# Attention and group norm of an audio tower kept transposed, and its planner re-priced

## The chip, the cores and the metric

The kernel runs on one core of one Trainium2 chip. The metric is the device time of one execution in microseconds (us), the median of three executions. Engines are named as in the profile: PE (matrix multiply), PEld (its weight loads), DVE (vector), ACT (activation functions), POOL, and SP, which only issues DMAs.

## The reference

A batch of 32 signals of 160000 samples is cut into 313 frames of 512 (a DCT turns each frame into 512 features). Then one layer of retention-like attention with a residual, and one feed-forward part (FFN) that sums sines and cosines, with a residual.

```python
h = frames @ dct.T                                   # 32 x 313 x 512
X = layernorm(h)
Q, K, V = xpos(X @ W_Q), xpos(X @ W_K), X @ W_V      # 8 heads of 64
p = softmax(Q @ K.T) * Dmat                          # Dmat: decay gamma ** |n - m|
Y = p @ V
Yn = (Y - mean(Y)) * rsqrt(var(Y) + 1e-5)            # group norm: over the 64 of one head
h = h + (silu(X @ W_G) * (Yn * gn_weight + gn_bias)) @ W_O
x = layernorm(h)
theta = x[..., None, :] / (1 + abs(W)) + B_param     # 256 units x 512 features
sin, cos = 4096-entry tables at round(theta * 4096 / 2pi)
out = (cos * attn_cos).sum(-1) @ proj_cos.T + (sin * attn_sin).sum(-1) @ proj_sin.T
h = h + silu(out)
```

The FFN needs a sine and a cosine for each of 32 x 313 x 256 x 512 arguments. That is the bulk of the work, and ACT computes them all (L636).

## The kernel before, in words

**The FFN.** Two sequences form a pair, and 16 pairs pass through a ring. The 256 units are 8 blocks of 32, and a *round* (`ffn_round`, L574) takes one block for all pairs that are in the ring. Pair p enters at round `STARTS[p]` (L33) and stays for 8 rounds, so rounds hold one to four pairs, that is r = 2 to 8 sequences; 42 rounds are needed. I call a round's share of one pair a pair-round; there are 16 x 8 = 128. A round has 128 items (32 units x 4 chunks of 128 features), and `SLOT` = 24 sequences' worth of items make one *slot*: for r = 2, 4, 6, 8 a slot takes 12, 6, 4 or 3 items. In a slot DVE makes integer table indices, one instruction an item (L612), shifts them by a quarter turn (L621) and masks both sets (L628). ACT takes two sines of 7512 elements (L636, tile `trig`, two buffers). After each sine PE does 24 matmuls with a 32-column stationary matrix `hot` into four column groups of a PSUM bank (`pa`, L658), summing over features. At a round's end DVE copies the banks out (`part`, L675) and SP stores them. The index tile `ix` has five buffers. The normalized input of the FFN goes through DRAM (`xT_d`) and is loaded per chunk into `xT` (two buffers).

**Attention** (`attention`, L302) handles one sequence at a time in one set of buffers (`A`); the first two sequences run side by side ahead of the FFN, in `A` and `B`. Frames are three overlapping tiles of 105 (`NT` = 3, `ROW0`). Stages: DCT rows (`rows`, L275), layer norm with an inverse root by Newton steps on POOL (`rsqrt`, L221: seed on DVE, 12 operations on POOL), transposes, values V into `x.h`, and Q, K with rotation per pair of heads (`rotary`). Then scores per head: PE, maximum and subtraction on DVE (L382, L385). One exponential follows over all heads (L400), or, where the FFN is narrow, 24 small ones with sums on ACT (L404). Then each head's 9 transposes into PSUM (L428), the decay product by DVE (L440), and PV: 9 matmuls a head, the probabilities stationary, 64 columns of V moving (L446), so that Y lies with frames on the partitions; per two heads a copy to `x.h` (L460). The group norm squares Y (L481, or L478 on ACT), sums per head on DVE (L486), makes the variance (L488 to L491), takes the root on POOL, and multiplies it in on DVE (L498). Y is transposed by PE (L269) and gets weight and bias (L509), is multiplied with the gate (L514), and goes through W_O (`rows`, L515) to the residual (L517) and the second norm. `output` (L528) finishes a sequence after its 8 rounds: rows with the projections, silu (L547), residual (L550). In narrow phases ACT instead of DVE does the copies (`eng`).

**What sets the order.** Nothing is ordered by the source order itself. Every step is given to `Plan.add` (L56) with a key, an engine, a price in ns, and the buffers read and written. `emit` (L63) walks through the engines in the planner's own time: an operation is ready when its forerunners have ended by their prices (plus `WAIT` 300, and `LAND` 2500 after a DMA), and of the ready ones of an engine that with the lowest key is issued. The resulting queues are fixed, and each engine goes through its own in order. Keys count slots: an FFN slot's key is its number (`key_of`, L794), its table loads stand 4 to 10 earlier. A sequence's attention is spread over a stretch of keys `times[i]` to `times[i+1]` that ends 8 slots before its pair enters (L797 to L804); within it the function `step` places each stage by a share of the whole (L309). A wrong price therefore puts an instruction too early or too late in a queue.

Of the kernel before, what the change touches and what calls it, by code (L numbers as in the profile page):

```python
# [15 lines left out]
AF = mybir.ActivationFunctionType  # L16
ALU = mybir.AluOpType
# [4 lines left out]
P = 128  # L22
HOP = 512
# [4 lines left out]
EPS = 1e-5  # L28
RING = 8
# [3 lines left out]
STARTS = (0, 4, 8, 10, 12, 14, 16, 18, 20, 22, 24, 26, 28, 30, 32, 34)  # L33
# [93 lines left out]
def tile_audio_tower(ctx: ExitStack, tc: tile.TileContext, t: dict, out: bass.AP):  # L127
# [23 lines left out]
    class Buffers:  # L151


        def __init__(self, name, pool, psum):
# [16 lines left out]
            self.h = sb("h", NT, HOP)  # L171
            self.xnT = sb("xnT", NC4, S)
# [11 lines left out]
            self.sq = wide[:, : NT * HOP].rearrange("p (i d) -> p i d", d=HOP)  # L184
            self.hres = self.sq
            self.aff = wide[:, NT * HOP : NT * HOP + NC4 * S].rearrange("p (c s) -> p c s", s=S)
# [8 lines left out]

            self.y = self.W[:, 3, : NT * 2 * DH].rearrange("p (i d) -> p i d", d=2 * DH)
# [24 lines left out]
    def rsqrt(plan, key, val, r, u, kv, kr, ku):  # L221
# [17 lines left out]
        plan.add(key, "POOL", 6000, newton, (kv,), (kr, ku))  # L239
# [24 lines left out]
    def transposed(plan, key, x):  # L264

        for c in range(NC4):
            def go(c=c):
                for i in range(NT):
                    nc.tensor.transpose(  # L269
                        x.W[:, c, ROW0[i] : ROW0[i] + N], x.h[:N, i, c * P : (c + 1) * P],  # L270
                        ident[:N, :N],
                    )
            plan.add(key, "PE", 800, go, x.rows_of, x.banks(c))

    def rows(plan, key, x, lhsT, src, r, order=range(NT), src_r=()):  # L275

        for c in range(NC4):
            k = x.load(plan, key, src[c], src_r)
            for to, i in enumerate(order):
                plan.add(  # L280
                    key, "PE", 880,
# [7 lines left out]
    def columns(plan, key, x, bank, src):  # L289
# [4 lines left out]
        for c in range(NC4):  # L294
            plan.add(
                key, "PE", 550,
# [5 lines left out]
    def attention(plan, keys, sq, x, eng, swap_m=None):  # L302
# [6 lines left out]
        def step(n=1.0):  # L309
            done[0] += n  # L310
            return keys(done[0] / 135.0)
# [14 lines left out]
        plan.add(step(0), "SP", DMA_NS, lambda: nc.sync.dma_start(x.u, t["frames"][sq]), (), us)  # L326
        rows(plan, step(7), x, x.u, t["dct"], us)
        copy(plan, step(), eng, NT * HOP, x.h[:N], W3, x.banks(0, 1, 2), hs)
        residual(step(0), False)
        layernorm(plan, step(3), x)  # L330
        transposed(plan, step(3), x)
        copy(plan, step(), eng, NC4 * S, x.xnT, x.W[:, :, :S], x.banks(0, 1, 2, 3), (x.k("xnT"),))


        rows(plan, step(7), x, x.xnT, wv_d, (x.k("xnT"),), range(NT - 1, -1, -1),
             ("wv_d",))
        copy(plan, step(), eng, NT * HOP, x.h[:N], W3, x.banks(0, 1, 2), hs)
        plan.add(step(0), "POOL", 500, lambda: nc.gpsimd.memset(x.h[0:1, : NT - 1, :], 0.0), (), hs)

        plan.add(step(0), "SP", DMA_NS, lambda: nc.sync.dma_start(x.table, t["turn_qk"]),  # L340
                 (), probs[-4:-2])

        def rotary(g):
            key = step(4)
# [7 lines left out]
            else:  # L352
                copy(plan, key, eng, 2 * S, x.raw, x.W[:, 0:2, :S], x.banks(0, 1), probs[-1:])
                for i in range(2):
                    plan.add(key, "PE", 550,
# [11 lines left out]
        def scores(hd):  # L367
            key = step(2.5)
            r0 = (hd % 2) * DH
            qk, kq = x.qk[hd // 2 % 2], x.k("u", hd // 2 % 2)  # L370
            for i in range(NT):
                plan.add(
                    key, "PE", 660,
# [34 lines left out]
        plan.add(step(2), "ACT", 18200 if eng == "ACT" else 9500, exps,  # L408
                 (), [*probs, x.k("sm"), x.k("lu")])
        if eng == "DVE":  # L410
            for a in range(0, H, 2):
                plan.add(step(0), "DVE", 2080,
# [4 lines left out]
        for hd in range(H):  # L417
            key = step(5)
# [4 lines left out]
            for jj in range(NT):  # L423
# [8 lines left out]
                plan.add(key, "PE", 800, go, (probs[a],), x.banks(jj))  # L432
# [10 lines left out]
            for i in range(NT):  # L443
                def go(i=i, hd=hd, a=a):
                    for jj in range(NT):
                        nc.tensor.matmul(  # L446
                            x.y[:N, i, (hd % 2) * DH : (hd % 2 + 1) * DH],
                            x.prob[:N, a, jj, ROW0[i] : ROW0[i] + N],
                            x.h[:N, jj, hd * DH : (hd + 1) * DH],
                            start=(jj == 0), stop=(jj == NT - 1),  # L450
                        )
                plan.add(key, "PE", 1000, go, (probs[a], hs[hd // 2]), x.banks(3))
            if hd % 2 == 0:
# [3 lines left out]
            h0 = hd - 1  # L457
            plan.add(
                step(), "DVE", 560,
                lambda h0=h0: nc.vector.tensor_copy(  # L460
                    x.h[:N, :, h0 * DH : (h0 + 2) * DH], x.y[:N]),
                x.banks(3), (hs[h0 // 2],),
            )


        key = step(6)
        for g in range(NC4):
            columns(plan, key, x, g, t["wg"][g])
        plan.add(step(), "ACT", 1270,
# [4 lines left out]
        xh = x.h[:N].rearrange("p i (h e) -> p (i h) e", e=DH)  # L474
        key = step(5)
        if eng == "ACT":
            plan.add(key, "ACT", 1500,
                     lambda: nc.scalar.activation(x.sq[:N], x.h[:N], AF.Square), hs, room)  # L478
        else:
            plan.add(key, "DVE", 1760,  # L480
                     lambda: nc.vector.tensor_tensor(x.sq[:N], x.h[:N], x.h[:N], ALU.mult),  # L481
                     hs, room)

        def variance():
            f = lambda tl: tl[:N].rearrange("p i h -> p (i h)")
            nc.vector.tensor_reduce(  # L486
                f(x.gv), x.sq[:N].rearrange("p i (h e) -> p (i h) e", e=DH), AX.X, ALU.add)
            nc.vector.reciprocal(f(x.sm), f(x.sm))  # L488
            nc.vector.tensor_tensor(f(x.gv), f(x.gv), f(x.sm), ALU.mult)
            nc.vector.tensor_tensor(f(x.gv), f(x.gv), f(x.sm), ALU.mult)  # L490
            nc.vector.tensor_scalar(f(x.gv), f(x.gv), 1.0 / DH, EPS, ALU.mult, ALU.add)  # L491
        plan.add(key, "DVE", 2700, variance, room, [x.k("gv"), x.k("sm")])
        rsqrt(plan, key, x.gv[:N], x.gr[:N], x.gu[:N], x.k("gv"), x.k("gr"), x.k("gu"))
        plan.add(key, "POOL", 300,
                 lambda: nc.gpsimd.tensor_tensor(x.gr[:N], x.gr[:N], x.sm[:N], ALU.mult),
                 (x.k("sm"),), (x.k("gr"),))
        plan.add(key, "DVE", 1760,
                 lambda: nc.vector.tensor_tensor(  # L498
                     xh, xh, x.gr[:N].rearrange("p i h -> p (i h)").unsqueeze(2).to_broadcast(
                         (N, NT * H, DH)), ALU.mult),  # L500
                 (x.k("gr"),), hs)


        transposed(plan, step(4), x)
        residual(step(0), True)
        key = step(2)
        for c in range(NC4):
            plan.add(key, "DVE", 530,
                     lambda c=c: nc.vector.tensor_scalar(  # L509
                         x.aff[:, c, :], x.W[:, c, :S], gnw[:, c : c + 1], gnb[:, c : c + 1],  # L510
                         ALU.mult, ALU.add),
                     x.banks(c), room)
        plan.add(key, "DVE", 1460,
                 lambda: nc.vector.tensor_tensor(x.u, x.u, x.aff, ALU.mult), room, us)  # L514
        rows(plan, step(7), x, x.u, t["wo"], us)  # L515
        plan.add(step(2), "DVE", 1760,
                 lambda: nc.vector.tensor_tensor(x.h[:N], x.h[:N], W3, ALU.add),  # L517
                 x.banks(0, 1, 2), hs)
        residual(step(0), False)
        layernorm(plan, step(3), x)  # L520
        transposed(plan, step(3), x)
        key = step()
# [51 lines left out]
    def ffn_round(plan, k0, blk, ring):  # L574
# [10 lines left out]
        for parts in slots:  # L585
# [45 lines left out]
            for k in (1, 0):  # L631
# [34 lines left out]
                plan.add(key, "PE", 150 * len(parts) * r, go,  # L666
# [32 lines left out]
    gnw = load("gnw", NC4)  # L699
# [128 lines left out]
def _constants(S):  # L828
# [35 lines left out]
    c["decay"] = dec.astype(f)  # L864
    return c
# [20 lines left out]
def _layout(x, W_Q, W_K, W_V, W_G, W_O, gn_weight, gn_bias, W, B_param, attn_cos, attn_sin, pc, psn):  # L886
# [14 lines left out]
    a["gnw"] = np.ascontiguousarray(gn_weight.reshape(NC4, P).T)  # L901
# [38 lines left out]
```

## Time and profile before

| | |
|---|---|
| times of three executions | 18586.4, 18587.15, 18591.35 us (median 18587.15) |
| profiled execution, its own time | 18593.15 us |
| its span, first to last instruction | 18591.2 us |
| sines (L636) | 2760, ACT busy 17398.1 us with them |
| FFN matmul records (L658) | 131072, two to a matmul |
| index, shift and mask (L612, L621, L628) | DVE busy 6499.2 + 2905.2 + 5581.8 us |
| granted PE clock, mean | 0.918 |

The page gives for each engine its busy time and its share of the span, then the same in 40 slices of 465 us, a digit being tenths of the slice. Groups of instructions are named by line, engine, operation, and `out<-in` with their tiles; after a count comes busy time and the mean of one in ns. A view by stage cuts the span where one asks and gives each engine's busy time with the number of its instructions in brackets, then granted PE clock, DMA share and GB/s. A line of waits reads: engine, what it was about to do, what released it, then us in total, times, and the longest.

### The profile page before, as it was taken

To read this page: it belongs to the slowest core of one execution; us is meant where nothing else is said; L and a number is where in the kernel's file an instruction comes from. 1 tells how busy PE (TensorE), PEld (TensorE's weight loads), DVE (VectorE), ACT (ScalarE), POOL (GpSimd) and SP (SyncE) were. 2 spreads that over 40 slices of the span, in tenths; PEclk is the share of its full clock that TensorE was granted. 3 is DMA by queue.
4 is the path that set the end of the run, shared out by engine and by line. 5 is a ranking of instruction groups with operands and counts; after the bars stand their busy time and mean duration, and the time that the engine had idled before them with its cause. 6 is when DMAs were issued, how large, how long until landed. Compare 5 with 4: busy or idle time off the path is not lost. (4 is left out here: it accounts for less than half of the span.)

```text
span 18591.2 us, 325962 instructions
## 1 busy us (share of the span) xinstructions
PE 14520.5 (78%) x148768; PEld 6791.6 (37%) x148768; DVE 17165.7 (92%) x11210; ACT 17827.2 (96%) x3248; POOL 968.9 (5%) x1222
## 2 busy tenths in 40 slices
PE   8788888888777877778877787877788777666666
PEld 5443333334333333333333333333333333222222
DVE  6989999999999999999999999999999999888887
ACT  4899999999999999999999999999999999999998
POOL 0000000000000000000000000000000000000000
PEclk8899999999999999999999999999999999888888
DMA  3221121121111111111111111111111111001011
GB/s 94 71 66 56 60 67 58 54 61 58 45 38 47 57 50 52 45 45 57 48 58 47 43 53 48 58 48 55 39 50 57 48 56 42 29 21 33 20 40 53
DMA packets 598691, 942.55 MB, mean 51 GB/s; under 512 B 116768, under 2 KB 337952, under 8 KB 586048
## 3 DMA queue, kind: packets, MB, share of 16 engines
q1 hardware_dynamic: 597312, 921.70, 16.0%
q8 instruction: 1166, 19.10, 0.4%
q14 instruction: 213, 1.74, 0.0%
HBM read 816.78 MB, written 104.66 MB: 50 GB/s over the span
## 5 line engine op out<-in xcount | busy, mean ns | idle before, releaser
L636 ACT ACTIVATE trig<-ix 128x7512 f32<-128x7512 int16 (+1 forms) x2760 | 17398.1, 6386 | 456.8 <-PE pa L658 229.7
L658 PE MATMUL pa<-trig,hot 128*32 128x313 f32 x131072 | 10304.5, 468 | 3545.1 <-ACT trig L636 3530.3
L658 PEld LDWEIGHTS pa<-trig,hot 128*32 128x32 f32 x131072 | 4291.2, 118 | 9312.4 <-ACT trig L636 4578.4
L612 DVE TENSOR_SCALAR ix<-xT,f 128x2504 int16<-128x2504 f32 (+3 forms) x5376 | 6499.2, 1268 | 431.6 <-ACT trig L636 389.4
L628 DVE TENSOR_SCALAR ix<-ix 128x15024 int16<-128x15024 int16 (+4 forms) x1656 | 5581.8, 3385 | 41.1
L621 DVE TENSOR_SCALAR ix<-ix 128x7512 int16<-128x7512 int16 (+1 forms) x1380 | 2905.2, 2105 | 356.1 <-ACT trig L636 264.4
L297 PE MATMUL a_W<-a_xnT,a_ring 128*128 128x313 f32 x4896 | 1426.2, 437 | 40.9 <-DVE a_prob L385 15.4
L282 PE MATMUL a_W<-a_ring,a_u 128*105 128x512 f32 x2256 | 1087.5, 625 | 141.2 <-DMA a_u<-in_frames 52.9
L297 PEld LDWEIGHTS a_W<-a_xnT,a_ring 128*128 128x128 f32 x4896 | 891.8, 190 | 580.1 <-issue 212.5
L282 PEld LDWEIGHTS a_W<-a_ring,a_u 128*105 128x105 f32 x2256 | 374.7, 177 | 756.3 <-issue 615.0
L233 POOL TENSOR_TENSOR a_gu<-a_gr 105x24 f32<-105x24 f32 x93 | 104.5, 1124 | 9461.6 <-DVE a_gr L227 9456.7
L446 PE MATMUL a_W<-a_h,a_prob 105*105 105x64 f32 x4464 | 483.0, 264 | 77.6 <-DVE a_prob L440 77.4
L374 PE MATMUL a_W<-a_u 64*105 64x313 f32 x1488 | 477.7, 453 | 72.1 <-DVE a_prob L385 40.0
L446 PEld LDWEIGHTS a_W<-a_h,a_prob 105*105 105x105 f32 x4464 | 447.3, 177 | 212.1 <-issue 143.7
L282 PE MATMUL a_W<-a_ring,a_xnT 128*105 128x512 f32 x744 | 350.6, 611 | 22.3 <-DVE a_xnT L219 20.5
L233 POOL TENSOR_TENSOR a_lu<-a_lr 105x3 f32<-105x3 f32 x186 | 141.1, 759 | 4073.3 <-DVE a_lr L227 4063.6
L374 PEld LDWEIGHTS a_W<-a_u 64*105 64x105 f32 x1488 | 234.0, 171 | 310.8 <-DVE a_prob L385 79.2
L428 PE MATMUL a_W<-ident,a_prob 105*105 105x105 f32 x2232 | 284.9, 272 | 44.1 <-DVE a_h L460 26.1
L382 DVE TENSOR_REDUCE a_mx<-a_W 105x3 f32<-105x939 f32 x248 | 280.1, 1130 | 37.6 <-PE a_W L374 36.5
L428 PEld LDWEIGHTS a_W<-ident,a_prob 105*105 105x105 f32 x2232 | 237.9, 178 | 159.4 <-issue 92.5
L440 DVE TENSOR_TENSOR a_prob<-a_W,a_u 105x939 f32<-105x939 f32 x248 | 279.8, 1128 | 16.3 <-PE a_W L428 10.9
L385 DVE TENSOR_TENSOR a_prob<-a_W,a_mx 105x939 f32<-105x939 f32 x248 | 281.7, 1136 | 8.5
(134 smaller groups left out, 3386.8 us busy)
## 6 DMA issues: line engine op xcount, KB each, us to landing
hot<-in_hot SPq DMA_DIRECT2D x1344, 128.0 KB
xT<-xT_d SPq DMA_DIRECT2D x88, 1252.0 KB
a_u<-in_decay SPq DMA_DIRECT2D x248, 260.5 KB
a_ring<-in_proj SPq DMA_DIRECT2D x128, 256.0 KB
a_ring<-in_dct SPq DMA_DIRECT2D x124, 256.0 KB
a_ring<-wv_d SPq DMA_DIRECT2D x124, 256.0 KB
a_ring<-in_wq SPq DMA_DIRECT2D x124, 256.0 KB
a_ring<-in_wk SPq DMA_DIRECT2D x124, 256.0 KB
```

Of the source, the lines that this page charges most:

```text
L282: lambda c=c, i=i, k=k, to=to: nc.tensor.matmul(x.W[:N, to, :], lhsT[:, c, ROW0[i] : ROW0[i] + N], x.ring[k], start=(c == 0), stop=(c == N ...
L297: lambda c=c: nc.tensor.matmul(x.W[:, bank, :S], w[:, c, :], x.xnT[:, c, :], start=(c == 0), stop=(c == NC4 - 1)),
L374: lambda i=i: nc.tensor.matmul(x.W[:N, i, :S], qk[r0 : r0 + DH, 0, ROW0[i] : ROW0[i] + N], qk[r0 : r0 + DH, 1, :], start=True, stop=True,),
L382: lambda: nc.vector.tensor_reduce(m[:N], x.W[:N, :NT, :S], AX.X, ALU.max),
L385: lambda: nc.vector.tensor_tensor(x.prob[:N, hd], x.W[:N, :NT, :S], m[:N].unsqueeze(2).to_broadcast((N, NT, S)), ALU.subtract),
L428: nc.tensor.transpose(x.W[:N, jj, ROW0[i] : ROW0[i] + N], x.prob[:N, a, i, ROW0[j] : ROW0[j] + N], ident[:N, :N],)
L446: nc.tensor.matmul(x.y[:N, i, (hd % 2) * DH : (hd % 2 + 1) * DH], x.prob[:N, a, jj, ROW0[i] : ROW0[i] + N], x.h[:N, jj, hd * DH : (hd + 1) ...
L612: nc.vector.tensor_scalar(ix[:, x[0], pt * r * S : (pt + 1) * r * S], now["xT", y][:, : r * S], f[:, 0, n : n + 1], f[:, 1, n : n + 1], AL ...
L621: nc.vector.tensor_scalar(ix[:, x[1], :E], ix[:, x[0], :E], float(LUT // 4), None, ALU.add)
L628: nc.vector.tensor_scalar(ix[:, i, :E], ix[:, i, :E], LUT - 1, LUT // 2, ALU.bitwise_and, ALU.bitwise_xor)
L636: nc.scalar.activation(tl[:, :E], ix[:, x[1 - k], :E], AF.Sin, bias=-PI32, scale=ANG)
L658: nc.tensor.matmul(now["pa", p][g * 32 : g * 32 + 32, :S], now["hot", hot[n // 4 * 4, c]][:, n % 4, k, :], now["trig", w][:, s0 : s0 + S], ...
```

## The change

Three things change together.

**Attention keeps Y transposed.** V is stored by pairs of heads (`x.v`). After both heads of a pair have their decayed probabilities, 6 matmuls make their result: V (105 x 64) is stationary, the probabilities (313 frames wide) move, and the two heads go to columns 0 to 63 and 64 to 127 of one PSUM bank. The copy (`x.yT`, 128 x 313) thus has features on the partitions. The group norm's sums come from PE with a 0/1 table `of_head` (12 matmuls, 8 columns wide). Two DVE operations make the variance, the softmax sum folded into the epsilon term. The root is computed on POOL as before, then PE transposes it (3), DVE copies it (8 x 313), and PE spreads it over the features with `head_w`, which holds `gn_weight` (4 matmuls). DVE multiplies, and adds the bias and multiplies the gate in one operation for each of 4 chunks. One of the three rounds of 12 transposes goes, and `gnw` too; two small tables are loaded per sequence.

**The planner's numbers.** The steps' shares come from `SHARE` and `TIMES`; prices change: Newton 6000 to 7500, three transposes 800 to 400, row matmuls 880 to 970, column matmuls 550 to 600, scores 660 to 640, the memset 500 to 2000. The FFN's PE operations get a key lower by 1.

**`STARTS`** changes, so that 43 rounds are needed.

```diff
+SHARE = dict(rows=5.0, copy=2.5, norm=8.0, turn=0.7, rotary=4.2, scores=3.2, exps=2.0, head=3.5,
+             pair=0.8, gate=4.1, silu=1.5, group=7.0, affine=5.0)
+TIMES = dict(rows=3, copy=5, norm=2, turn=4, rotary=4, scores=8, exps=1, head=8, pair=4, gate=1,
+             silu=1, group=1, affine=1)
+WHOLE = sum(SHARE[k] * TIMES[k] for k in SHARE)
...
-STARTS = (0, 4, 8, 10, 12, 14, 16, 18, 20, 22, 24, 26, 28, 30, 32, 34)
+STARTS = (0, 4, 7, 9, 11, 13, 15, 17, 19, 21, 23, 25, 27, 29, 32, 35)
...
+            self.v = flat.rearrange("p (g j d) -> p j g d", g=NC4, j=NT)
+            self.yT = flat.rearrange("p (g s) -> p g s", g=NC4)[:, :, :S]
...
-        plan.add(key, "POOL", 6000, newton, (kv,), (kr, ku))
+        plan.add(key, "POOL", 7500, newton, (kv,), (kr, ku))
...
-            plan.add(key, "PE", 800, go, x.rows_of, x.banks(c))
+            plan.add(key, "PE", 400, go, x.rows_of, x.banks(c))
...
-        def step(n=1.0):
-            done[0] += n
-            return keys(done[0] / 135.0)
+        def step(stage=None):
+            if stage:
+                done[0] += SHARE[stage]
+            return keys(done[0] / WHOLE)
...
-                plan.add(key, "PE", 800, go, (probs[a],), x.banks(jj))
+                plan.add(key, "PE", 400, go, (probs[a],), x.banks(jj))
...
-            for i in range(NT):
-                def go(i=i, hd=hd, a=a):
-                    for jj in range(NT):
-                        nc.tensor.matmul(
-                            x.y[:N, i, (hd % 2) * DH : (hd % 2 + 1) * DH],
-                            x.prob[:N, a, jj, ROW0[i] : ROW0[i] + N],
-                            x.h[:N, jj, hd * DH : (hd + 1) * DH],
-                            start=(jj == 0), stop=(jj == NT - 1),
-                        )
-                plan.add(key, "PE", 1000, go, (probs[a], hs[hd // 2]), x.banks(3))
...
+            def go(g=hd // 2):
+                for jj in range(NT):
+                    for b in range(2):
+                        nc.tensor.matmul(
+                            x.W[b * DH : (b + 1) * DH, 3, :S],
+                            x.v[:N, jj, g, b * DH : (b + 1) * DH],
+                            x.prob[:N, 2 * g + b, jj, :], start=(jj == 0), stop=(jj == NT - 1))
+            plan.add(key, "PE", 1900, go, (*probs[hd - 1 : hd + 1], hs[hd // 2]), x.banks(3))
+            plan.add(step("pair"), "DVE", 550,
+                     lambda g=hd // 2: nc.vector.tensor_copy(x.yT[:, g, :], x.W[:, 3, :S]),
+                     x.banks(3), (hs[hd // 2],))
...
-                     lambda: nc.vector.tensor_tensor(x.sq[:N], x.h[:N], x.h[:N], ALU.mult),
+                     lambda: nc.vector.tensor_tensor(x.sqT, x.yT, x.yT, ALU.mult), hs, room[:2])
+        def sums():
+            for i in range(NT):
+                for c in range(NC4):
+                    nc.tensor.matmul(x.W[:N, 0, i * H : (i + 1) * H],
+                                     x.sqT[:, c, ROW0[i] : ROW0[i] + N], x.of_head[:, c, :],
+                                     start=(c == 0), stop=(c == NC4 - 1))
+        plan.add(key, "PE", 2400, sums, room, x.banks(0))
...
-            nc.vector.tensor_reduce(
-                f(x.gv), x.sq[:N].rearrange("p i (h e) -> p (i h) e", e=DH), AX.X, ALU.add)
-            nc.vector.reciprocal(f(x.sm), f(x.sm))
-            nc.vector.tensor_tensor(f(x.gv), f(x.gv), f(x.sm), ALU.mult)
-            nc.vector.tensor_tensor(f(x.gv), f(x.gv), f(x.sm), ALU.mult)
-            nc.vector.tensor_scalar(f(x.gv), f(x.gv), 1.0 / DH, EPS, ALU.mult, ALU.add)
+            nc.vector.scalar_tensor_tensor(f(x.gv), f(x.sm), EPS, f(x.sm), ALU.mult, ALU.mult)
+            nc.vector.scalar_tensor_tensor(
+                f(x.gv), x.W[:N, 0, : NT * H], 1.0 / DH, f(x.gv), ALU.mult, ALU.add)
...
-                 lambda: nc.gpsimd.tensor_tensor(x.gr[:N], x.gr[:N], x.sm[:N], ALU.mult),
-                 lambda: nc.vector.tensor_tensor(
-                     xh, xh, x.gr[:N].rearrange("p i h -> p (i h)").unsqueeze(2).to_broadcast(
-                         (N, NT * H, DH)), ALU.mult),
-        transposed(plan, step(4), x)
+        def factors():
+            for i in range(NT):
+                nc.tensor.transpose(x.W[:H, 1, ROW0[i] : ROW0[i] + N], x.gr[:N, i, :], ident[:N, :N])
+        plan.add(step("turn"), "PE", 400, factors, (x.k("gr"),), x.banks(1))
+        plan.add(step(), "DVE", 500,
+                 lambda: nc.vector.tensor_copy(x.rT, x.W[:H, 1, :S]), x.banks(1), (room[1],))
+        def spread():
+            for c in range(NC4):
+                nc.tensor.matmul(x.W[:, c, :S], x.head_w[:, c, :], x.rT, start=True, stop=True)
+        plan.add(step("turn"), "PE", 2400, spread, room[1:], x.banks(0, 1, 2, 3))
+                 lambda: nc.vector.tensor_tensor(x.sqT, x.yT, x.W[:, :, :S], ALU.mult),
...
-                         x.aff[:, c, :], x.W[:, c, :S], gnw[:, c : c + 1], gnb[:, c : c + 1],
-                         ALU.mult, ALU.add),
-                 lambda: nc.vector.tensor_tensor(x.u, x.u, x.aff, ALU.mult), room, us)
+                     lambda c=c: nc.vector.scalar_tensor_tensor(
+                         x.u[:, c, :], x.sqT[:, c, :], gnb[:, c : c + 1], x.u[:, c, :],
+                         ALU.add, ALU.mult),
...
-                plan.add(key, "PE", 150 * len(parts) * r, go,
+                plan.add(key - 1, "PE", 150 * len(parts) * r, go,
```

## The prediction

> **What bounds the kernel now.** I read the page's busy time first, then busy time by stage, then the waits of the stage that loses most. The stages are cut at the first sine (316.1 us) and at the last `part` copy (L675) of rounds 0, 13, 33 and 41.
>
> ```profile
> PE 14520.5 (78%) x148768; PEld 6791.6 (37%) x148768; DVE 17165.7 (92%) x11210; ACT 17827.2 (96%) x3248; POOL 968.9 (5%) x1222
> ...
> DVE  6989999999999999999999999999999999888887
> ACT  4899999999999999999999999999999999999998
> ```
>
> ACT carries 17827 us in a span of 18591.2: its 764 us of idle time are all that can be won, since the change leaves the sines alone.
>
> ```profile
> core 0: us, PE busy (x) PEld busy (x) DVE busy (x) ACT busy (x) POOL busy (x), PEclk, DMA share, GB/s
> 0.00:316.10 316.10, 265.07 (x992) 171.67 (x992) 144.84 (x178) 51.42 (x124) 19.96 (x82) 0.79 0.35 107
> 316.10:481.40 165.30, 137.60 (x1241) 67.75 (x1244) 163.03 (x193) 147.91 (x26) 6.41 (x13) 0.93 0.23 69
> 481.40:4576.10 4094.70, 3328.88 (x32913) 1624.26 (x32906) 3904.80 (x3127) 3824.48 (x802) 284.09 (x379) 0.92 0.20 62
> 4576.10:15796.20 11220.10, 8942.89 (x92956) 4182.35 (x92955) 10592.72 (x6201) 11092.43 (x1858) 658.47 (x748) 0.93 0.16 49
> 15796.20:18542.00 2745.80, 1819.89 (x20624) 736.43 (x20624) 2356.78 (x1513) 2708.06 (x437) 0.00 (x0) 0.88 0.10 32
> 18542.00:18591.20 49.20, 26.17 (x48) 9.17 (x48) 3.51 (x2) 2.90 (x2) 0.00 (x0) 0.78 0.35 99
> ```
>
> Span less ACT busy: 265 us idle before the first sine (PE busy 84%), 17 in round 0, 270 in rounds 1 to 13 (the early stage), 128 in rounds 14 to 33, 38 in the tail, 46 at the end. In the early stage DVE is the busiest engine. Its waits there:
>
> ```profile
> DVE a_h L257 <- POOL a_lr L236: 35.9, 20, 2.9
> DVE ix L621 <- ACT trig L636: 24.6, 14, 5.0
> DVE a_h L498 <- POOL a_gr L495: 20.3, 9, 2.9
> DVE ix L612 <- DMA xT<-xT_d: 19.4, 1, 19.4
> ```
>
> It hardly waits for ACT: DVE sets the pace. Later ACT does, and what it loses there goes mostly to PE:
>
> ```profile
> ACT trig L636 <- PE pa L658: 56.0, 43, 8.8
> ACT trig L636 <- issue: 48.5, 13, 6.5
> ```
>
> [...] a sine's 24 L658 matmuls (128x32, 313 wide) take 3.37 us, 0.14 each, against 0.64 for an unsplit 313-wide one (L374: 477.7 us / 744). [...] a Newton step on `a_gr` takes 0.21 to 0.24 us at 234 us, but L233 averages 1.12 over the run. [...]
>
> **The change, step by step.** Durations are busy time over count in the profile before (the mean of one where they don't overlap). Counts per round come from the DVE queues as built.
>
> *DVE work of one attention.* Goes: L460 4 x 0.55, L481 1.75, L486 1.75, L488 to L491 0.84, L498 1.76, L509 4 x 0.54, L514 1.46: 11.9 us. Comes: four copies 128x313 at 0.48 (L675) 1.9, the square 1.46 (L514), two 24-wide ops 0.4 (L489), the 8x313 copy 0.48, the product from PSUM 1.46 (L360), four 128x313 `scalar_tensor_tensor`. No row shows that form: [...] 0.60 (L509), taken 0.53, 2.1. Sum 7.8, so -4.1 us (-3.9 to -4.3).
>
> *STARTS.* The index work of a round per pair it holds (L612 0.527/0.861/1.196/1.525 us for 2/4/6/8 sequences, L621 2.126, L628 4.072 a slot) is 134.8, 122.0, 117.9 and 115.6 us for 1, 2, 3, 4 pairs; ACT needs 135.9 (17398/128). So narrow rounds put DVE level with ACT before any attention. Up to the first 28 pair-rounds, rounds 1 to 13 before hold 3 of one pair, 6 of two, 4 of three; rounds 1 to 12 after hold 3, 4, 4 and 1 of four. Index work: 3282 to 3257; attention in between (10 sequences): 676 to 635. DVE 3959 to 3891; ACT stays near 3845, so DVE stays the limit, narrowly. Before, the stage took 4095, 136 more than DVE's work.
>
> *POOL priced at 7500, the factor off DVE's path.* DVE work queued between seed and L257 averages 7.5 us, its wait 1.6 (100.1/62): the round trip is 9.1. After, 8.4 to 11.4 are queued in the early stage; the `a_gr` reader, now the 8x313 copy, has 8.8 to 11.9, but behind PE's three transposes. Of 56 us of POOL waits I keep 15: -41 (0 to -56).
>
> *Round 4's start.* Before, sequence 3's last norm stands just ahead of round 4's first index: DVE waits 19.4 us for xT, ACT 13.4 for the index. In the queue after, its `wo` rows, residual, norm and transposes all stand there: 12 row matmuls at 0.96 (L282), 11.5, and Newton, some 4 us at POOL's undisturbed pace, lie bare, then the same 19. DVE loses about 23 more (0 to 35). At later starts 26 us of DVE work or more lie between last copy and first index; 11 were enough before.
>
> *New waits.* DVE's second variance op (L508 after) waits for PE's sums, with 3.2 to 3.8 us of DVE work mostly queued between it and the square. The sums take some 2.4 us, plus 3.4 if a sine's matmuls stand ahead: 0 to 2.6 us of wait, taken 1, ten times: +10 (0 to 26). Queued behind it on DVE are the index ops, for which ACT waits. PE's three transposes wait for `a_gr`; two sines' matmuls (12.7 us of ACT) are mostly queued between sums and transposes, more than the 9.1 us of the round trip, so the sine behind them isn't held: nothing, or 1 us an attention without that cover.
>
> Early stage, with the 136 us of waits and gaps of before: 3891 + 136 - 41 + 23 + 10 = 4019, against 4095: **-76** (-30 to -140).
>
> *PE in rounds 14 to 33.* Per attention PV goes from 72 matmuls at 0.216 (L446), 15.6 us, to 24 at 0.30 if halves overlap, 7.2 (0.64, 15.4, if not). Twelve transposes (0.14) go; 12 sums (about 0.2, as L446), 4 spreads (0.6) and 3 transposes come: +3.5 net. Beside the sines this is cover: a sine lasts 6.37 us (17122.8/2688), its matmuls 3.37, so PE has 3 us spare. What counts is how much attention work stands between two sines' matmuls. I priced each stretch of attention matmuls in the two PE queues as above and summed what exceeds 3 us: from sine 720 on, 204 us before, 82 after (the FFN's PE key less 1, and PE prices near the trace, break the stretches up). Scaling ACT's 56 us by 82/204: **-34** (-50 to 0) in rounds 14 to 33. The 48.5 us of "issue" I leave, and DVE's 2 us per sequence won there are under ACT's cover.
>
> *Before the first sine* PE is the path: one head's PV takes 3.3 us until 219 us, 1.8 after (16 heads about 46 us). Eight pairs at 3.0 or 1.8 make 22. Of 24 us I take **-18** (-24 to 0: DVE or the new chain sums, Newton, transpose, spread may become last). Round 0: 3 us less DVE: **-2**.
>
> *Tail.* A third round of one pair, whose index work leaves ACT about 1 us; rounds 38 to 41 lost 5 to 8 us each two: **+8** (0 to +12). Fewer and shorter ACT squares: -2. The two table loads sit on SP's queue far ahead of use, and the memset and v's regrouped copy keep their sizes: nothing, or 1 us of SP issue.
>
> Sum: -76 - 34 - 18 - 2 + 8 - 2 = **-124**. The profiled execution took 18593.15 us (span 18591.2, 2 around it), 6 above the median 18587.15. 18587 - 124 = 18463, say **18460**.
>
> **Rivals.**
> *Waits melt further* (better prices align queues everywhere): early stage 3891 + 41 (round 4) + 20, mid-stage PE waits gone: another -67 and -22: **18370**. For: ACT waits on PE 140.7 us in the early stage. Against: DVE's work alone is above ACT's there.
> *The halves don't overlap*: no gain ahead of the first sine, none in the mid stage: 18460 + 18 + 34 = **18512**. For: fp32, 64 wide, is not in this trace. Against: the 32-wide groups overlap.
> *DVE waits for PE instead* (slower): transposes are priced 3 x 400 instead of 3 x 800, so DVE's `decayed` and the score reduction are queued close behind PE, whose queue holds a sine's 3.4 us in front. Sixteen such waits per attention, ten attentions: 160 in the early stage, where each us of DVE is a us of span. At 0.78 us more each, the 124 are gone; at 1.3, 208 us, it ends at **18668**. Against: today L440 and L382 lose 12 us there in all, and nine transposes cost 9 x 0.128 = 1.15 us, what the new price says.
>
> **Chances.** Forecast .58 (own range 18380 to 18520), melting .18, no overlap .10, PE waits .14, half of it within 0.2% (37 us, about what a measurement can tell from no change). Faster .86, same .07, slower .07. Range 18330 to 18560: it leaves out the low end of melting and the upper half of the PE waits, some 1 in 10, because the unknown costs (halves, 0.53, round 4, the new waits) add up to about 90 us either side.
>
> **What would show it.** Early stage (to the end of round 12) near 4020 us with POOL waits under 20; one DVE wait of 35 to 45 us ahead of round 4; first sine near 298 us; ACT's waits on PE after round 13 near 22; PV group 1.8 us a pair. Wrong if waits of `decayed` on PE grow to tens of us, or the stage ends at ACT's 3845.

## The result and the profile after

The changed kernel takes 18546.9 us (median of 17; 18529.4 to 18565.3), the kernel before 18587.15: 0.9978 of it (95% interval 0.9972 to 0.9985), 40 us less. The forecast was 18460, 127 less: sign and range hold, the size is three times too large. Two executions ran at a lower granted PE clock than all the others (0.91 to 0.93), one of experiment 2 (19706.91 us at 0.734) and one of experiment 6 (18750.21 us at 0.841), and the medians below leave both out. The profiled execution's own time is 18546.9 us, its span 18544.8, so the two spans differ by 46.4.

The page's busy times and slices, after:

```profile
PE 14447.6 (78%) x146432; PEld 6507.7 (35%) x146432; DVE 17071.9 (92%) x11244; ACT 17819.3 (96%) x3246; POOL 1050.9 (6%) x1190
...
DVE  6989999999999999999999999999998999988888
ACT  4889999999999999999999999999999999999998
```

DVE lost 94 us of work, as intended. POOL has 32 instructions fewer and is busy 82 us longer: this is the first sign of what went wrong. Busy time by stage, cut like before at the first sine and at the last `part` copy (now L698) of round 0, of the round that completes 28 pair-rounds (now round 12), of round 32, and of the last round:

```profile
core 0: us, PE busy (x) PEld busy (x) DVE busy (x) ACT busy (x) POOL busy (x), PEclk, DMA share, GB/s
0.00:312.20 312.20, 244.56 (x846) 136.02 (x846) 137.24 (x174) 50.84 (x124) 18.04 (x80) 0.83 0.37 108
312.20:480.60 168.40, 140.45 (x1216) 68.31 (x1217) 166.55 (x195) 148.38 (x26) 8.32 (x13) 0.89 0.24 66
480.60:4529.20 4048.60, 3309.58 (x32173) 1540.73 (x32172) 3835.60 (x2951) 3819.66 (x800) 335.73 (x357) 0.92 0.21 61
4529.20:15607.60 11078.40, 8742.41 (x90049) 3928.57 (x90047) 10342.66 (x6035) 10940.73 (x1831) 638.70 (x691) 0.93 0.17 49
```

The early stage took 4048.6 us instead of 4094.7: DVE's work in it fell by 69 us (3904.8 to 3835.6), but its gaps grew by 23 (189.9 to 213.0). The later rounds can't be matched by number, since `STARTS` moved them; by pair-rounds done they can (`part` copies of the timelines):

| us | before | after | difference | forecast |
|---|---|---|---|---|
| to the first sine | 316.1 | 312.2 | -4 | -18 |
| round 0 | 165.3 | 168.4 | +3 | -2 |
| to pair-round 28 (the early stage) | 4094.7 | 4048.6 | -46 | -76 |
| pair-rounds 28 to 96 | 9539 | 9551 | +12 | about -34 |
| pair-rounds 96 to 128 | 4427 | 4415 | -12 | +8 |

The waits of DVE in the early stage, the longest:

```profile
DVE a_h L268 <- POOL a_lr L247: 28.9, 18, 2.3
DVE a_prob L519 <- PE a_W L516: 21.8, 9, 3.3
DVE a_h L540 <- PE a_W L293: 21.0, 4, 12.8
DVE ix L644 <- ACT trig L659: 13.3, 15, 2.3
```

The wait of the group norm for POOL is gone from DVE, 20.3 us before. In its place DVE waits 21.8 us at the 8x313 copy (L519) for PE. Over all of DVE's lines, its waits on POOL there fell from 56.2 to 28.9, on PE they rose from 35.8 to 94.7. The waits of ACT from pair-round 28 to the end of round 32:

```profile
ACT trig L659 <- issue: 100.5, 22, 7.1
ACT trig L659 <- PE pa L681: 28.1, 16, 5.2
```

The waits on PE melted from 56.0 to 28.1, near the 22 of the forecast. But "issue" grew from 48.5 to 100.5 and took it all back. And over the whole run PE has a new wait:

```profile
PE pa L681 <- ACT trig L659: 3539.1, 1864, 21.7
PE a_W L516 <- POOL a_gr L247: 92.7, 28, 5.7
```

L516 is the transposes of the group norm's factors: PE stands before them 28 times (there are 32 attentions) and waits for POOL. One attention, at 8265 us, shows what stands behind them. POOL's timeline (start, duration, instruction; in brackets the idle time before it and what ended it):

```profile
8271.40 2.02 POOL L244 TENSOR_TENSOR a_gu<-a_gr 105x24 f32<-105x24 f32 x1 [340.84 <-DVE a_gr L238]
8273.50 2.08 POOL L245 TENSOR_TENSOR a_gu<-a_gu,a_gv 105x24 f32<-105x24 f32 x1
8275.67 1.95 POOL L246 TENSOR_SCALAR a_gu<-a_gu 105x24 f32<-105x24 f32 x1
8277.71 1.44 POOL L247 TENSOR_TENSOR a_gr<-a_gr,a_gu 105x24 f32<-105x24 f32 x1
8279.23 1.41 POOL L244 TENSOR_TENSOR a_gu<-a_gr 105x24 f32<-105x24 f32 x1
8280.71 1.42 POOL L245 TENSOR_TENSOR a_gu<-a_gu,a_gv 105x24 f32<-105x24 f32 x1
8282.22 0.21 POOL L246 TENSOR_SCALAR a_gu<-a_gu 105x24 f32<-105x24 f32 x1
8282.52 0.24 POOL L247 TENSOR_TENSOR a_gr<-a_gr,a_gu 105x24 f32<-105x24 f32 x1
```

DVE's timeline beside it:

```profile
8271.23 2.11 DVE L644 TENSOR_SCALAR ix<-ix 128x7512 int16<-128x7512 int16 x1
8273.38 4.18 DVE L651 TENSOR_SCALAR ix<-ix 128x7512 int16<-128x7512 int16 x2
8277.48 4.56 DVE L635 TENSOR_SCALAR ix<-xT,f 128x2504 int16<-128x2504 f32 x3
8284.55 0.47 DVE L519 COPY a_prob<-a_W 8x313 f32<-8x313 f32 x1 [2.51 <-PE a_W L516]
```

Each of POOL's first six operations ends with a DVE instruction: one beside the shift (2.11), two beside the two masks (2.09 each), three beside the three index instructions (1.52 each). When DVE stands still at 8282.0, the other six (two of them shown) take 0.21 to 0.24 us. The twelve need 12.6 us (8271.40 to 8283.99); at the undisturbed pace, 0.31 from start to start, they would need 3.7, an estimate. It is no exception: of the 19 roots from pair-round 28 to the end of round 32, 18 take 12.6 to 13.0 us. The same operation on `a_gu` (L246) took 1.95 us beside a mask of 2.09 and 0.21 beside nothing; what ties the two engines together, no run shows. The timelines of PE and of ACT show who pays:

```profile
8277.04 3.37 PE L681 MATMUL pa<-trig,hot 128*32 128x313 f32 x48 [1.34 <-ACT trig L659]
8284.05 0.47 PE L516 MATMUL a_W<-ident,a_gr 105*8 105x105 f32 x3 [3.64 <-POOL a_gr L247]
8285.08 4.54 PE L523 MATMUL a_W<-a_prob 8*128 8x313 f32 x8 [0.56 <-DVE a_prob L519]
8289.55 8.98 PE L681 MATMUL pa<-trig,hot 128*32 128x313 f32 x96
```

```profile
8264.19 25.51 ACT L659 ACTIVATE trig<-ix 128x7512 f32<-128x7512 int16 x4
8295.49 12.83 ACT L659 ACTIVATE trig<-ix 128x7512 f32<-128x7512 int16 x2 [5.80 <-issue]
```

PE is done with a sine at 8280.4, stands 3.64 us, then transposes, waits for DVE's copy and spreads. The matmuls of the next sine, which ACT finished at 8283.3 (8264.19 and three times 6.38), begin at 8289.55. `trig` has two buffers, so ACT stands 5.80 us from 8289.7. The profile finds no releaser for it and calls it "issue".

The standstill is not all that PE loses. The spread (L523) takes 4.54 us here, at a granted clock of 0.50, and the two sines behind it 8.98 us at 0.72, where one took 3.37 at 1.00 just before. Of the 19 spreads from pair-round 28 to the end of round 32, nine take 4.54 us at 0.50, each behind a wait of PE for POOL of 3.64 to 4.43 us. The other ten, behind 0 to 2.86 us of that wait, take 2.37 to 4.27 at 0.54 to 1.00; the one without any (14038.29) takes 2.37 at 1.00. The spread of the attention shown in experiment 1 below takes 2.37, too (8223.17). The longer standstill and the lower clock go together here; which brings which, no run separates.

### The profile page after: what moved, and what is told of

Read it like the earlier page. It is cut to its first block, busy times and chain, and to the rows that moved or that the text cites. A ratio compares the mean times of both kernels' runs of the same rounds, so it can differ in the third digit from the quotient of the medians.

```text
span 18544.8 us, 321896 instructions
## 1 busy us (share of the span) xinstructions
PE 14447.6 (78%) x146432; PEld 6507.7 (35%) x146432; DVE 17071.9 (92%) x11244; ACT 17819.3 (96%) x3246; POOL 1050.9 (6%) x1190
## 5 line engine op out<-in xcount | busy, mean ns | idle before, releaser
L644 DVE TENSOR_SCALAR ix<-ix 128x7512 int16<-128x7512 int16 (+1 forms) x1379 | 2903.9, 2106 | 618.3 <-ACT trig L659 536.0
L388 PE MATMUL a_W<-a_u 64*105 64x313 f32 x1488 | 466.3, 445 | 71.6 <-DVE a_prob L399 59.8
L442 PE MATMUL a_W<-ident,a_prob 105*105 105x105 f32 x2232 | 284.3, 272 | 97.4 <-DVE a_prob L454 63.3
L388 PEld LDWEIGHTS a_W<-a_u 64*105 64x105 f32 x1488 | 231.9, 169 | 305.0 <-DVE a_prob L399 93.1
L454 DVE TENSOR_TENSOR a_prob<-a_W,a_u 105x939 f32<-105x939 f32 x248 | 280.1, 1129 | 43.0 <-PE a_W L442 34.1
L442 PEld LDWEIGHTS a_W<-ident,a_prob 105*105 105x105 f32 x2232 | 235.3, 177 | 237.5 <-issue 143.1
L396 DVE TENSOR_REDUCE a_mx<-a_W 105x3 f32<-105x939 f32 x248 | 280.1, 1130 | 40.8 <-PE a_W L388 40.0
L465 PE MATMUL a_W<-a_prob,a_h 105*64 105x313 f32 x1488 | 232.9, 449 | 23.4 <-DVE a_prob L454 23.3
L374 DVE TENSOR_TENSOR a_prob<-a_W,a_prob 128x1252 f32<-128x1252 f32 x124 | 180.6, 1457 | 45.3 <-PE a_W L370 37.3
```

Source lines behind the costliest of these rows:

```text
L388: lambda i=i: nc.tensor.matmul(x.W[:N, i, :S], qk[r0 : r0 + DH, 0, ROW0[i] : ROW0[i] + N], qk[r0 : r0 + DH, 1, :], start=True, stop=True,),
L396: lambda: nc.vector.tensor_reduce(m[:N], x.W[:N, :NT, :S], AX.X, ALU.max),
L442: nc.tensor.transpose(x.W[:N, jj, ROW0[i] : ROW0[i] + N], x.prob[:N, a, i, ROW0[j] : ROW0[j] + N], ident[:N, :N],)
L454: nc.vector.tensor_tensor(x.prob[:N, a], x.W[:N, :NT, :S], w3, ALU.mult)
L644: nc.vector.tensor_scalar(ix[:, x[1], :E], ix[:, x[0], :E], float(LUT // 4), None, ALU.add)
```

## The experiments

Differences are between medians, ratios to the kernel before carry their 95% interval.

**1. The root on DVE.** The 12 operations of the group norm's root go to DVE's queue, with a price of 2500.

```diff
-        plan.add(key, "POOL", 7500, newton, (kv,), (kr, ku))
+        plan.add(key, "DVE" if dve else "POOL", 2500 if dve else 7500, newton, (kv,), (kr, ku))
...
-        rsqrt(plan, key, x.gv[:N], x.gr[:N], x.gu[:N], x.k("gv"), x.k("gr"), x.k("gu"))
+        rsqrt(plan, key, x.gv[:N], x.gr[:N], x.gu[:N], x.k("gv"), x.k("gr"), x.k("gu"), True)
```

> The changed kernel, with the 12 Newton operations of the group norm's root on DVE instead of POOL (price 2500 ns; the layer norms' stay on POOL). Theory A ([...] the root is late whatever is queued, PE waits in front of its transposes and ACT behind PE): PE's wait for a_gr vanishes, DVE's wait for the transposes falls from 72 us to under 20, ACT's idle time from the end of round 12 to 15608 us falls from 138 us to about 50; DVE gets 31 x 2.3 = 71 us of work, 23 of it in the early stage in place of 22 us of waits there. Time about 18450 to 18480. Theory B (those ACT gaps have another cause, such as missing records or the frames' DMA): mid stage unchanged, early stage longer by 20: 18550 to 18575.

Measured: 18417.43, ratio 0.9908 (0.9895 to 0.9921): 129 us below the kernel after, though DVE works 66 us more (17138.0). DVE's timeline of one root, the first and last operation, and the transposes on PE:

```profile
8212.57 0.18 DVE L245 TENSOR_TENSOR a_gu<-a_gr 105x24 f32<-105x24 f32 x1
...
8214.95 0.18 DVE L248 TENSOR_TENSOR a_gr<-a_gr,a_gu 105x24 f32<-105x24 f32 x1
```

```profile
8212.02 3.37 PE L682 MATMUL pa<-trig,hot 128*32 128x313 f32 x48 [0.20 <-ACT trig L660]
8215.32 0.43 PE L517 MATMUL a_W<-ident,a_gr 105*8 105x105 f32 x3
```

The root takes 2.6 us instead of 12.6 and is ready while PE works on one sine. ACT's waits from pair-round 28 to round 32, which were 100.5 and 28.1:

```profile
ACT trig L660 <- PE pa L682: 28.3, 16, 4.8
ACT trig L660 <- issue: 5.8, 2, 4.7
```

So all but 6 us of this "issue" was the root. ACT's waits on PE stayed as they were, and the stretch is 100 us shorter (11078.4 to 10978.0).

**2. The root stays on POOL, but with room.** Only its price goes from 7500 to 24000, so the planner queues four or five sines on PE ahead of the transposes instead of two.

```diff
-        rsqrt(plan, key, x.gv[:N], x.gr[:N], x.gu[:N], x.k("gv"), x.k("gr"), x.k("gu"))
+        rsqrt(plan, key, x.gv[:N], x.gr[:N], x.gu[:N], x.k("gv"), x.k("gr"), x.k("gu"), 24000)
```

> The changed kernel, with only the planner's price of the group norm's Newton raised from 7500 to 24000 ns, so that 4 to 5 sines' matmuls instead of 2 stand between PE's sums and its transposes, and 10 to 20 DVE instructions instead of 5 between seed and the 8x313 copy. Theory A: the root is ready in time, waits vanish as in e1 without DVE work: 18440 to 18470. Theory A', that DVE instructions in between are what slows POOL and 11 of them are not enough for 12 operations: part of it, about 18500. Theory B: unchanged, 18540 to 18555.

Measured: 18458.8, ratio 0.9931 (0.9918 to 0.9944), 88 below the kernel after. PE's wait for POOL, over the whole run:

```profile
PE a_W L516 <- POOL a_gr L247: 5.0, 3, 1.8
```

So the loss lies not in the engine that computes the root, but in PE's standing in front of it. POOL's steps are even slower here (L245 on `a_gu` 1390 ns on average, 1045 after), and it doesn't matter. The gain is 41 us smaller than in experiment 1: the first sine comes 9 us later, at 320.9, and 31.4 us of "issue" are left from pair-round 28 to the end of round 32, whose cause no run separates.

**3. One refinement instead of three.** This leaves out two thirds of the group norm's refinement of the root: 4 operations on POOL instead of 12. The price stays 7500, so the planner issues everything in the order of the kernel after.

```diff
-            for _ in range(3):
+            for _ in range(steps):
...
-        rsqrt(plan, key, x.gv[:N], x.gr[:N], x.gu[:N], x.k("gv"), x.k("gr"), x.k("gu"))
+        rsqrt(plan, key, x.gv[:N], x.gr[:N], x.gu[:N], x.k("gv"), x.k("gr"), x.k("gu"), 1)
```

> The changed kernel with one Newton iteration instead of three for the group norm's root, still on POOL (4 operations instead of 12; it leaves out two thirds of the root's refinement). If each POOL operation lasts about as long as the DVE instruction beside it, 4 operations end within the 5 DVE instructions that stand between seed and copy: PE's wait for a_gr falls from 93 us to under 15 and the time to 18430 to 18470. If POOL's start or the hand-over to PE is what is slow, whatever the number of operations: above 18520.

Measured: 18446.7, ratio 0.9923 (0.991 to 0.9935), 100 below the kernel after. The costliest groups of POOL on `a_gu` in it, and PE's wait:

```profile
L246 POOL TENSOR_SCALAR a_gu<-a_gu 105x24 f32<-105x24 f32 x31 | 66.6, 2148 | 2.7
L245 POOL TENSOR_TENSOR a_gu<-a_gu,a_gv 105x24 f32<-105x24 f32 x31 | 60.2, 1943 | 2.4
```

```profile
PE a_W L516 <- POOL a_gr L247: 6.5, 10, 2.1
```

These two operations take a DVE instruction's time, 1.9 to 2.1 us on average, but there are only four in all: PE's wait falls from 92.7 to 6.5 us. Fewer operations are enough, on the same engine and in the same queues. ("Issue" is 30.4 us from pair-round 28 to the end of round 32.)

**4. Both roots on DVE.** As in 1, the layer norms' too.

```diff
+        rsqrt(plan, key, x.lv[:N], x.lr[:N], x.lu[:N], x.k("lv"), x.k("lr"), x.k("lu"), True)
```

> Both norms' Newton operations on DVE. Against the group norm's alone (18417): DVE gains 62 x 2.0 = 124 us of work, 40 of it in the early stage, and loses 78 us of waits for POOL, 30 of them there; ahead of the first sine the roots are 2 to 3 us shorter twice. 18400 to 18430. If it is slower by more than 10 us, DVE's work in the early stage outweighs the waits; POOL is then the right place for the layer norm.

Measured: 18429.65, ratio 0.9913 (0.9899 to 0.9926): nothing more to win. It is 12 us above experiment 1, but their executions overlap (18414.81 to 18442.96, and 18413.69 to 18421.04), so whether it is slower stays open. DVE has 17255.7 us of work, 118 more than in experiment 1. PE's wait for the layer norm (L281 for DVE's L269) falls from 66.7 to 10.8 us, and the time doesn't fall with it: either that wait held no sine, or DVE's added work takes the gain back. No run separates the two.

**5. The kernel before with its root on DVE,** and with it the multiplication of the root by the softmax sums that follows.

```diff
-        plan.add(key, "POOL", 6000, newton, (kv,), (kr, ku))
+        plan.add(key, "DVE" if dve else "POOL", 2500 if dve else 6000, newton, (kv,), (kr, ku))
...
-        plan.add(key, "POOL", 300,
-                 lambda: nc.gpsimd.tensor_tensor(x.gr[:N], x.gr[:N], x.sm[:N], ALU.mult),
+        plan.add(key, "DVE", 200,
+                 lambda: nc.vector.tensor_tensor(x.gr[:N], x.gr[:N], x.sm[:N], ALU.mult),
```

> The kernel before with the group norm's Newton operations and the multiplication after them on DVE. There DVE itself, not PE, waits for that root, 69 us in all, 20 in the early stage; it gets 31 x 2.5 = 78 us of work instead, 25 there. If the loss comes only from PE standing in front of the root, as the change made it: no gain, 18580 to 18600. If POOL's slow root costs as much in the kernel before: 18480 to 18530.

Measured: 18570.5, ratio 0.999 (0.9984 to 0.9997): 19 us below the runs of before beside it (18589.16), a little more than "no gain". The same edit of the root is worth 129 in the kernel after. POOL's root was slow before, too; but there DVE waited for it, here PE does.

**6. The new `STARTS` alone, and all but them.**

```diff
-STARTS = (0, 4, 8, 10, 12, 14, 16, 18, 20, 22, 24, 26, 28, 30, 32, 34)
+STARTS = (0, 4, 7, 9, 11, 13, 15, 17, 19, 21, 23, 25, 27, 29, 32, 35)
```

> The kernel before with the new STARTS and nothing else. Without STARTS the changed kernel took 18569, with them 18547. My sum (26 us less index work in the early stage, 8 more in the tail): about 18570. Rival: they pay only together with the cheaper attention, since the earlier start of the third pair needs it: 18590 or more.

> The changed kernel with the STARTS of before (42 rounds). My sum gave the new STARTS 26 us of index work and 0.2 us less ACT in the early stage, less the third round of one pair at the end (8 us) and a worse start of round 4 (23 us): about nothing to -18. Rival: the new STARTS are what made the early stage shorter at all, since attention alone saves less than the new waits cost: 18590 or more.

Measured: before with the new `STARTS` 18535.34, ratio 0.9971 (0.996 to 0.9982), 54 us below the runs of before beside it (18589.16); the kernel after with the old ones 18569.1 (13 executions, 18549.7 to 18586.9), 17 us below the runs of before beside it (18586.4; 28 executions, 18576.9 to 18602.4). So neither outcome that was expected for the old ones came: the rest of the change is worth 17 us with the old `STARTS`. With the new ones it costs some 12 (18535 to 18547; the intervals of the two ratios overlap), and `STARTS` alone gives no less than the whole change.

**7. `STARTS` in two parts,** on the kernel before: the early pairs one round sooner (the tail as it was), or the last two pairs further apart (the beginning as it was).

```diff
+STARTS = (0, 4, 7, 9, 11, 13, 15, 17, 19, 21, 23, 25, 27, 29, 31, 33)
...
+STARTS = (0, 4, 8, 10, 12, 14, 16, 18, 20, 22, 24, 26, 28, 30, 33, 36)
```

> The kernel before with the third and all later pairs one round earlier (0, 4, 7, 9, ... 31, 33), the tail's spacing unchanged. STARTS as a whole gave 54: 21 up to pair-round 28, 17 more to pair-round 96, the rest in the tail. If the parts are separate: 18587 - 38 = 18549. By the prediction's sum (index work -26, nothing later): 18561. Rival: the whole gain is the shift's: 18535.

> The kernel before with only the last two pairs further apart (... 28, 30, 33, 36), so 44 rounds. The prediction priced the longer tail at +8: 18595. The profile of the new STARTS alone shows some 15 to 19 us won after pair-round 96: 18570, if that is the tail's spacing. Rival: it is the shift's phase: 18587.

Measured: 18554.06, ratio 0.9982 (0.9975 to 0.999), and 18569.86, ratio 0.9991 (0.9985 to 0.9998): -33 and -17, together -51, near the -54 of both at once. The longer tail, priced at +8, is a gain.

**8. The root on DVE with the old `STARTS`.** The edits of experiment 1, and the old tuple put back.

> The group norm's root on DVE, with the old STARTS. If the gain of STARTS (54 us on the kernel before) is its own and adds to that of the root: 18417 + 54 = 18471; with what it was worth in the kernel after (18569.4 - 18546.9 = 23): 18440. Rival: STARTS only gave time back that the root's waits had taken, so that with the root on DVE nothing is left of it: 18417.

Measured: 18426.86, ratio 0.9911 (0.9896 to 0.9926), 9 above experiment 1. `STARTS` is worth 54 on the kernel before, 22 on the kernel after, 9 with the root out of the way. From pair-round 28 to 96 the kernel before takes 9539 us, with the new `STARTS` 9522, with the root on DVE 9452 (old `STARTS`) and 9454 (new): there it had only given back time that the waits had taken. ACT's waits from pair-round 28 to the end of round 33 in this run:

```profile
ACT trig L660 <- PE pa L682: 31.0, 16, 5.4
ACT trig L660 <- ACT trig L660: 3.8, 6, 1.0
```

There is no "issue" at all in this stretch.

**9. The FFN's key not lowered.**

```diff
-                plan.add(key - 1, "PE", 150 * len(parts) * r, go,
+                plan.add(key, "PE", 150 * len(parts) * r, go,
```

> The changed kernel without the FFN matmuls' key of 1 less. I credited the key and the PE prices together with ACT's waits on PE after round 13 (56 to 28 us). If the key does it: 18565 to 18590, with ACT's waits on PE back above 45 us there. If the prices do it, within 10 us of 18547.

Measured: 18544.57, ratio 0.9977 (0.9969 to 0.9985): as the kernel after. The key does nothing that can be measured. From pair-round 28 to the end of round 32 "issue" stays at 85.7 us and ACT's waits on PE at 31.4, so it isn't the key that melted them from 56.0.

**10. Sequence 2's frames later,** on experiment 1.

```diff
-        plan.add(step(), "SP", DMA_NS, lambda: nc.sync.dma_start(x.u, t["frames"][sq]), (), us)
+        plan.add(step(), "SP", DMA_NS, lambda: nc.sync.dma_start(x.u, t["frames"][sq]), (("xT_d", 1),) if sq == 2 else (), us)
```

> The kernel with the group norm's root on DVE, and sequence 2's frames loaded only after sequence 1's normalized FFN input has been stored. In the kernel after, PE stood 8.9 us before sequence 2's first DCT rows, whose DMA had not landed, and the second sequence's last transposes were queued behind them; its last copy to b_u came at 287.8 us though b_h had been ready at 278.7. If that queueing is what holds the first sine: the copy near 282, the first sine 5 to 6 us earlier than the 309.6 of the root on DVE (near 304), and the whole 3 to 6 us shorter, near 18413. Rival: the later frames make sequence 2 late and round 1 or 2 gives it back: first sine near 304, whole unchanged at 18417 or above.

Measured: 18413.93, ratio 0.9906 (0.9892 to 0.9919). ACT's timeline:

```profile
282.53 1.20 ACT L228 COPY b_u<-b_W 128x1252 f32<-128x1252 f32 x1 [5.09 <-PE b_W L281]
...
305.76 25.53 ACT L660 ACTIVATE trig<-ix 128x7512 f32<-128x7512 int16 x4 [0.77 <-DMA a_ring<-wv_d]
```

The copy comes when expected, the first sine 3.8 us sooner (309.6 in experiment 1) instead of 5 to 6; in the whole time it can't be told from experiment 1, so its two outcomes stay undecided. The best kernels of the study are this one and experiment 1.

## Why the prediction was right and wrong

**What held.** DVE's work in the early stage: forecast 3959 to 3891, 68 less; measured 69 less. Both of its ends are some 55 too high (3904.8 and 3835.6 in the traces), so the 136 us of waits and gaps that the sum carried along were really 189.9; only the difference was right. The two halves of PV do overlap: twelve records (6 matmuls) of L465 take 1.80 us, 0.30 a matmul, as I had estimated, against 0.64 for an unsplit one (L374 before), so that rival is out. ACT's waits on PE in the later rounds: 22 forecast, 28 measured, though the planner's key had no part in it (experiment 9), and prices and cheaper attention are not separated. DVE's wait at L508 for PE's sums: +10 forecast, 2.7 measured, inside its bounds. The slower rival, sixteen waits of DVE at its decay product and reduction, did not come: L454 on L442 and L396 on L388 cost 5.0 and 9.5 us in the early stage, against 12 in all before. Nor did the waits melt further, as the faster rival had it: the early stage ended above its forecast.

**The step that failed** is the one on the new waits: "two sines' matmuls (12.7 us of ACT) are mostly queued between sums and transposes, more than the 9.1 us of the round trip, so the sine behind them isn't held: nothing". Both of its numbers were wrong, for one reason each.
- 9.1 was not a round trip of POOL. It was the layer norm's: the DVE work queued before that reader (L257) plus its wait, on the average of all sequences. But POOL advances by about one operation per DVE instruction, so its time depends on what DVE does meanwhile: 12.6 us in the attention shown, 3.7 at the undisturbed pace. The mean of L233 quoted in the prediction, 1.12 us against 0.21 to 0.24, already said so; the step treated it as a constant.
- The cover was not 12.7 us. In the attention shown PE finished the sums at 8270.6 and the second sine's matmuls at 8280.4: 9.8 us, since ACT had finished the first of the two sines just then (8270.6), and only the second cost a whole sine's time. It then reached the transposes 3.6 us before the root did.

Without cover I had allowed 1 us an attention. PE stood 2.9 on average (92.7 / 32), and ACT up to 7.1 at a time, since PE's transposes, the copy on DVE and the spread (4.5 us) come on top before the next sine's matmuls. Experiment 1 takes just this away: the kernel is 129 us faster than the kernel after, and 118 faster than `STARTS` alone (18535 to 18417). The attention and price terms of my sum, -124 less the -26 and +8 that I had put down to `STARTS`, make -106. That is near the 118, but in part by luck: with the old `STARTS` the same comparison gives 160 (18587 to 18427). The runs do show the sign and the order of size of what a late root took back.

**Where it shows in the sum.**
- *Early stage,* -76 forecast, -46 measured. The POOL term, -41, was -27 (56.2 to 28.9), and DVE's waits on PE went up by 59 instead of 10: at the copy after the transposes 21.8, the rest in many smaller places. With the root on DVE all these waits on PE fall from 94.7 to 48.9.
- *Round 4's start,* +23 forecast. The wait for xT was 10.8 instead of 19.4, but DVE stood 12.8 for the `wo` rows before it and 4.9 for `part` copies and the norm: 28.5 in all, not the 35 to 45 looked for. ACT stood 22.0 us before that sine instead of 13.4: about +9.
- *Rounds 14 to 33,* -34 forecast: the 28 us won on PE were lost to "issue", which I "left" at 48.5 and which doubled. Much of it was the same root before: with the root on DVE "issue" is 20.5 us in the kernel before.
- *`STARTS`,* mis-sized: -18 forecast, -54 measured on the kernel before. The early shift gave -33 instead of -26, the tail -17 instead of +8. For the tail I counted only that narrow rounds leave ACT little slack; that the last attentions are spread over more rounds, I left out. The runs show that the spacing does it, not which of its effects.
- *Before the first sine,* -18 forecast, -4 measured, inside its bounds. The square of sequence A's group norm came 28 us sooner (229.7 to 201.4), its last copy 10.7 (282.8 to 272.1), B's only 2.3 (290.1 to 287.8), and it is B's that counts. Of B's delay experiment 10 gives back 4 us (286.9 in experiment 1 to 282.5): PE stood in front of rows whose frames had not landed. That the rest is the longer chain of sums, root, transposes and spread is read from the timelines, and no run separates it.

## What to carry to other kernels

When a result of POOL moves from a DVE reader to a PE reader, ask what is queued behind that reader: here a waiting DVE cost little, and a PE that waited between two sines' matmuls made ACT wait. Beside a DVE that works without pause, a chain of small POOL operations took about one DVE instruction for each operation, not its own durations; twelve on POOL (12.6 us) were beaten by twelve on DVE (2.6 us), though DVE was the busier engine. And where two edits win back the same idle time, their gains don't add: 54 us of `STARTS` were 9 once the root was in time.

## What the runs showed of the hardware that was not expected

- POOL operations of 105x24, 0.21 to 0.24 us beside an idle DVE, last 1.4 us beside 1.5 us index instructions and 2.0 us beside 2.1 us shifts and masks, in step with them. These don't slow DVE: L644 takes 2.11 us beside them (8271.23), and the same shift in experiment 1, where DVE computes the root, 2.12. A long POOL instruction may: in the kernel after, an L644 that starts at 9053.10, while a POOL memset (L352) of 5.30 us runs until 9053.88, takes 2.75.
- Four `scalar_tensor_tensor` of 128x313 in fp32 take 1.91 us (0.48 each), in the attention shown. The prediction took 0.53, an estimate of mine below the 0.60 measured at L509 before.
- Two fp32 matmuls with 64 stationary columns each, 313 wide, in one bank: 0.30 us each (six in 1.80 us, at a granted clock of 1.00), against 0.64 for an unsplit one (L374 before). Twice before the first sine six took 3.40, at a granted clock of 0.50.
- In the attention shown, the four fp32 matmuls (313 wide) that follow PE's standstill take 4.54 us at a granted clock of 0.50, against 2.37 at 1.00 at 14038.29, where PE had not waited for POOL.
